# A new order and new engines for the same operations in a one-core matmul kernel

## The chip, the cores and the metric

The kernel runs on one core of one Trainium2 chip. The metric is device time in microseconds (us) of one execution; lower is better. The engines are named as the profile names them: PE (TensorE, matmuls), PEld (its weight loads), DVE (VectorE), ACT (ScalarE), POOL (GpSimd), SP (SyncE, which here only issues DMAs). SBUF is the on-chip memory, PSUM the banks that PE writes its results to.

## The reference

For 4 batch rows of 1024 tokens with 512 features, in float32:

```
hidden   = concat(cond, cond)                              # (4, 512)
fused    = concat(x, mean_over_tokens(x), hidden)          # (4, 1024, 1536)
out      = x + relu(fused @ W + b)                         # W: (1536, 512)
```

Mean and hidden do not depend on the token, so for batch row r the matmul splits into `x @ W[0:512]` and one bias row `mean(x_r) @ W[512:1024] + cond_r @ (W[1024:1280] + W[1280:1536]) + b`.

## The kernel before, in words

**Products.** Tokens are cut into 32 tiles of 128 (t0 to t31, eight to a batch row). Each float32 operand is split into a rounded high part (`hi`, `w_hi`) and the rest (`lo`, `w_lo`), and a tile's result is the sum of hi\*w_hi, lo\*w_hi and hi\*w_lo over four blocks j of 128 features: 12 matmuls of 128x512 into one PSUM bank (`p{t}.{j}`, line 366; t31 goes in two halves of 256 columns, 24 matmuls). In the order table `p0.2.1` is one of the three alone, n = 0, 1, 2 in the order above. Tile t uses bank t mod 5, so tile t+5 needs tile t's bank emptied.

**Units.** The x operand has to be transposed. Tiles come in units u0 (t0), u1 (t1), u2 (t2, t3) and then u3 to u9 of four tiles. The first three are transposed by PE (`T`, line 261) from a regrouped copy (`y`, lines 237 and 239); from u3 on DVE transposes (`T`, line 263) what a DMA `Z{u}.{i}` brought into `z`: two of the four blocks into PSUM (`px`), the odd two into SBUF (`xT`). Then ACT writes `h` (the high part, and its sum over tokens, line 270), and `l` writes the rest, xT or px minus hi (line 276), on DVE or POOL; POOL cannot take the px blocks. The weights are split the same way (`wh`, `wl`, lines 218 to 224).

**Bias of a batch row r.** ACT scales the folded condition weights (`g`), POOL adds them up (`d`), ACT copies that into the PSUM tile `acc` (`as`). POOL turns the sums over tokens into means (`to`, lines 308 to 311); DVE adds mean times weight in four steps (`m{r}.0` to `m{r}.3`, line 320); then ACT `f`, DVE `fa`, ACT `vh`, DVE `vl` (lines 328 to 340) fold and split the result, one matmul `pb{r}` (line 344) sums it over partitions, and ACT copies it to `bias` (`bc`, line 348). `pb{r}` stands in PE's own stream between products: if `vl{r}` is late, PE waits.

**After the products.** Tiles t0 to t11: `K` empties the bank (ACT or DVE), `b` adds the bias in SBUF (line 437). Tiles t12 to t27: DVE's `K` empties the bank and adds the bias (line 441). Then `r` is the relu (line 446 on DVE, 448 on ACT), `F` adds x (line 455, DVE or POOL), `S` stores the tile. Tiles t28 to t31: `P` puts the bias into the bank beforehand, and DVE's `F` (lines 404, 424) does relu and sum from PSUM in one operation.

**What sets the order.** The string `ORDER` lists every operation once; `@d`, `@a`, `@p` give the engine (DVE, ACT, POOL) where there is a choice. The kernel is recorded in this order, each engine runs its own operations strictly in it, and waits go in from the data and buffers used. All DMAs but the first two of the weights go through SP in the order of the table, so an SP issue that waits holds the ones behind it.

Of the kernel before, what the change touches and what calls it, by code (L numbers as in the profile page):

```python
# [19 lines left out]


ORDER = """
W0@a fill W1@a X0.0 X0.1 W2 fill relu fill W3 fill X0.2 fill Z3.1 fill y0.1@d y0.0@p y0.2@p fill T0.0 wh0r@d Z3.2
T0.1 T0.2 wh0l@d h0.0 fill wl0r@p fill y1.0@d y1.1@a T0.3 l0.0@d fill h0.2 wl0l@p fill h0.1 T1.2 T1.0 p0.0.1 T1.1
wh1@d Z3.3 T1.3 p0.0.0 h1.0 p0.0.2 Z3.0 h1.3 l1.0@d p1.0.2 wl1@p h1.2 l0.1@d p1.0.0 l1.3@d wh2@a p0.1.0 p1.0.1 wh3@d
h1.1 p0.1.1 p0.2.0 h0.3 l0.2@d wl2@p C p1.2.0 l1.1@d p1.3.1 V p0.3.0 p1.1.0 B y3.0@d y2.0@a p1.3.0 p0.2.1 Z4.0
l1.2@d p1.1.1 wl3@d p1.1.2 p0.2.2 T2.2 Z4.2 T2.3 p1.2.1 h2.2 T2.0 T2.1 l2.2@d p0.3.2 Z4.3 h2.0 p1.2.2 p3.2 h2.3
l2.0@d h2.1 l2.3@d p2.0 l2.1@d Z4.1 l0.3@d p2.3 p2.2 T3.0 p3.1 T3.3 h3.0 T3.1 p3.0 h3.3 l3.0@d p2.1 h3.1 l3.3@p t3
p3.3 T3.2 M1 K2@d p1.3.2 l3.1@p M0 p0.3.1 K1@a p4.0 t2 M2 h3.2 p0.1.2 ac0@p p6.0 M3 l3.2@d K0@a p4.3 Z5.2 t0 K3@d
p5.3 t1 Z5.3 ac1@d g0.0 p7.2 p6.2 d0.0 Z5.0 g0.1 p5.2 d0.1 g1.0 p5.0 Z5.1 T4.1 T4.3 p5.1 d1.0 T4.2 p6.3 K5@a Z6.0  # L30
T4.0 as0 p4.2 to0 g1.1 p7.3 Z6.3 h4.1 m0.0 p6.1 g2.0 l4.1@p m0.1 p4.1 Z6.2 h4.2 m0.2 p7.1 K4@a m0.3 h4.3 p7.0 Z6.1
K6@a p8.1 l4.3@p l4.2@d h4.0 X4.1 p10.1 f0 Z7.2 d1.1 p9.1 fa0 Z7.1 p10.3 l4.0@d vh0 d2.0 p8.2 g2.1 vl0 Z7.0 p11.2
K7@a T5.3 d2.1 p11.3 T5.2 h5.3 Z7.3 p8.0 T5.0 l5.3@p T5.1 pb0 p10.0 bc0@a h5.0 p10.2 b1@p h5.1 X1.1 l5.0@d p9.3 X2.0
h5.2 b2@d p9.0 as1 Z8.2 to1 p9.2 r1@a l5.1@p l5.2@d p12.3 r2@a X1.0 m1.0 K9@a p8.3 Z8.0 F1@p T6.3 p11.0 T6.1 h6.3
p12.2 b0@p m1.1 h6.1 p12.0 T6.2 K8@a p12.1 b3@p g3.0 T6.0 p11.1 K10@a m1.2 Z9.3 h6.2 d3.0 p13.1 Z8.3 m1.3 h6.0 p14.0
Z8.1 l6.0@d f1 b4@p p13.3 r0@a l6.2@d p14.1 r3@a T7.2 l6.3@p p15.0 fa1 Z9.2 p13.0 T7.0 vh1 F2@p p15.1 K11@a vl1 X5.0
p13.2 F0@d Z9.0 b6@p p15.2 S1 T7.3 pb1 X5.1 l6.1@p p14.3 bc1@a as2 p14.2 K13 F3@p r6@a p16.0 K12 h7.3 p15.3 K14 h7.2
l7.3@p T7.1 p17.0 b5@d h7.1 p19.3 b9@p h7.0 p17.3 r4@a l7.0@d p19.2 to2 g3.1 l7.2@d F4@p p16.2 r5@a m2.0 p18.3 K15
b8@p S4 p18.2 Z9.1 m2.1 p16.3 X3.1 d3.1 m2.2 p19.0 m2.3 p18.1 F5@p T8.0 p16.1 f2 fa2 p20.3 b11@p S5 T8.3 S2 p17.2
vh2 X3.0 h8.0 vl2 p17.1 F6@p X2.1 h8.3 S3 T8.2 p19.1 l7.1@d b7@p S6 p20.0 X4.0 pb2 S0 p18.0 bc2@a l8.3@p X7.0 h8.2  # L40
p20.2 K17 r7@a p20.1 K16 as3 F7@p p22.2 T8.1 l8.0@d p21.3 h8.1 T9.0 S7 r8@a p21.1 l8.1@p X6.1 K19 r11@a p22.1 r9@a
l8.2@d b10@p p22.0 r14@a K18 p21.2 r13@a T9.1 h9.0 p24.2 F13@p T9.2 h9.1 p24.1 T9.3 h9.2 F8@p F9@d p21.0 r15@a p24.0
r10@a F11@p S8 K20 h9.3 p22.3 S13 K21 r17@a p23.1 X6.0 to3 r21@a p23.0 F10@p m3.0 r18@a p23.3 r20@a m3.1 p26.1
l9.3@p m3.2 p25.0 K22 F21@p p23.2 m3.3 r22@a p26.2 F15@p f3 S21 p24.3 S11 r12@a fa3 p27.3 S10 F17@p K23 S15 vh3
p25.1 S9 r16@a vl3 p25.2 r19@a F16@p r23@d p26.0 l9.0@d p25.3 F19@p S16 pb3 X7.1 p26.3 bc3@a S17 F12@p P28 p27.1 K25
p27.2 l9.2@d P30 F18@p p28.2 F14@d r25@a p30.2 l9.1@p K26 p28.0 S14 S18 F25@d P31l p27.0 S19 F23@p r26@a p30.0 K24
S25 p31.2l F26@p S23 K27 p31.0l r24@a S12 p31.1l P29 p31.3l F20@p p30.3 P31r F31l F22@d S31l p29.1 S26 p28.1 S20
r27@d S22 p29.0 F24@d F27@p p28.3 p29.3 F28 S24 p30.1 S27 S28 p29.2 F30 p31.1r F29 S30 p31.0r p31.3r S29 p31.2r F31r
S31r
""".split()  # L50


# [437 lines left out]
```

## Time and profile before

| | |
|---|---|
| median of 3 runs | 102.46 us (102.29 to 104.08) |
| the profiled execution | 102.85 us, span 101.1 us |
| PE busy | 95.8 us (95%), 427 matmuls |
| DVE / ACT / POOL busy | 79.3 / 60.6 / 80.0 us |
| HBM | 18.88 MB read, 8.39 MB written |

The span runs from the first instruction to the last; 1.75 us of the profiled execution lie around it. Matmuls overlap, so PE's busy share does not tell whether it lost time: the step from one matmul's start to the next one's does.

### The profile page before, as it was taken

The page shows a single profiled execution, that of the slowest core. Times are in us where ns is not written, and L with a number is a line of the kernel's source. Part 1 is how long each engine was busy: PE and PEld are TensorE (multiplying, and loading weights), DVE is VectorE, ACT ScalarE, POOL GpSimd, SP SyncE. Part 2 cuts the span into 40 slices and gives each one's busy share as a digit, 9 for nine tenths or more (in the row PEclk, how much of TensorE's full clock was granted, in tenths as well). Part 3 has the DMA queues.
Part 4 walks back from the last instruction along what each step waited for, and adds up shares of the span by engine and source line. Part 5 has one row for each costly group of instructions (what it writes and reads, how often), then busy time and mean ns, then how long its engine had stood idle before and what let it go on. Part 6 is the DMA issues. An engine that isn't in the chain of part 4 may idle for free.

```text
span 101.1 us, 1437 instructions
## 1 busy us (share of the span) xinstructions
PE 95.8 (95%) x427; PEld 76.4 (76%) x427; DVE 79.3 (78%) x129; ACT 60.6 (60%) x150; POOL 80.0 (79%) x77
## 2 busy tenths in 40 slices
PE   6999999999999999999999999999999998999940
PEld 2476888888888888888878888888878885898840
DVE  1257658984897889987999999989859799969930
ACT  2574545844996698993597327499955786350000
POOL 5359000969769899999999999999899999999700
PEclk9999999999999999999999999999999999999999
DMA  2999999999999999999999999999999759998894
GB/s 46 372 343 227 210 211 316 205 205 322 207 199 191 210 223 197 206 260 298 241 225 209 207 254 307 265 359 408 405 397 400 274 219 345 282 403 328 310 381 161
DMA packets 25345, 27.36 MB, mean 271 GB/s; under 512 B 1397, under 2 KB 15993, under 8 KB 25338
## 3 DMA queue, kind: packets, MB, share of 16 engines
q1 hardware_dynamic: 25050, 26.75, 102.6%
q10 hardware_dynamic: 288, 0.52, 1.5%
q8 instruction: 3, 0.05, 0.2%
q14 instruction: 4, 0.03, 0.1%
HBM read 18.88 MB, written 8.39 MB: 270 GB/s over the span
## 4 chain that ended last, share of the span: by engine, by line
PE 38%; DMA 23%; POOL 18%; DVE 10%; ACT 4%; issue 2%; ACTq 1%; SPq 1%; POOLq 0%
PE po L366 37%; DMA z<-in_x_dram 9%; POOL x L455 8%; DMA x<-in_x_dram 8%; DMA x<-in_L_cond_W_dram 6%; POOL lo L276 4%; POOL o L437 4%; DVE acc L320 2%; DVE lo L276 2%; ACT hi L270 2%; DVE w_hi L220 1%; DVE o L446 1%; POOL cond L302 1%; DVE o L441 1%; PE px L261 1%
## 5 line engine op out<-in xcount | busy, mean ns | idle before, releaser
L366 PE MATMUL po<-w_hi,lo 128*128 128x512 f32 (+1 forms) x132 | 50.7, 387 | 0.5 <-DVE lo L276 0.4
L366 PE MATMUL po<-w_hi,hi 128*128 128x512 f32 (+1 forms) x132 | 50.2, 385 | 0.0
L366 PE MATMUL po<-w_lo,hi 128*128 128x512 f32 (+1 forms) x132 | 50.1, 385 | 0.0
L455 POOL TENSOR_TENSOR x<-o,x 128x512 f32<-128x512 f32 x22 | 30.0, 1385 | 0.7 <-DVE o L446 0.4
L366 PEld LDWEIGHTS po<-w_hi,lo 128*128 128x128 f32 x132 | 24.8, 188 | 6.1 <-DVE lo L276 0.8
L366 PEld LDWEIGHTS po<-w_hi,hi 128*128 128x128 f32 x132 | 24.8, 188 | 5.4 <-DVE o L441 0.6
L366 PEld LDWEIGHTS po<-w_lo,hi 128*128 128x128 f32 x132 | 24.7, 188 | 5.0 <-ACT hi L270 0.3
L276 POOL TENSOR_TENSOR lo<-xT,hi 128x512 fp32r<-128x512 f32 x13 | 17.7, 1367 | 9.2 <-ACT hi L270 9.2
L448 ACT ACTIVATE o<-o 128x512 f32<-128x512 f32 x26 | 15.2, 622 | 4.0 <-DVE o L441 3.4
L437 POOL TENSOR_TENSOR o<-o,bias 128x512 f32<-128x512 f32 x10 | 13.9, 1390 | 0.0
L276 DVE TENSOR_TENSOR lo<-px,hi 128x512 fp32r<-128x512 f32 (+2 forms) x20 | 11.5, 588 | 2.2 <-ACT hi L270 2.2
L270 ACT ACTIVATE hi<-px 128x512 fp32r<-128x512 f32 (+2 forms) x20 | 10.3, 517 | 4.8 <-DVE px L263 2.5
L320 DVE SCALAR_TENSOR_TENSOR acc<-w_mean,tot,acc 128x512 f32<-128x512 f32 x16 | 12.0, 748 | 1.4 <-POOL tot L311 1.1
L441 DVE TENSOR_TENSOR o<-po,bias 128x512 f32<-128x512 f32 x16 | 10.5, 679 | 1.6 <-POOL x L455 1.4
L263 DVE STREAM_TRANSPOSE xT<-z 128x512 f32<-128x512 f32 x14 | 9.4, 687 | 2.2 <-POOL cond L302 2.2
L263 DVE STREAM_TRANSPOSE px<-z 128x512 f32<-128x512 f32 x14 | 9.5, 699 | 2.0 <-DMA z<-in_x_dram 1.8
L270 ACT ACTIVATE hi<-xT 128x512 fp32r<-128x512 f32 x14 | 8.7, 624 | 1.8 <-DVE xT L263 1.7
L455 DVE TENSOR_TENSOR x<-o,x 128x512 f32<-128x512 f32 x6 | 7.2, 1194 | 0.0
L298 ACT ACTIVATE term<-wc,cT 128x512 f32<-128x512 f32 x8 | 5.7, 718 | 2.2 <-DVE cT L284 1.4
L433 ACT ACTIVATE o<-po 128x512 f32<-128x512 f32 x10 | 5.9, 590 | 0.8 <-PE po L366 0.8
L302 POOL TENSOR_TENSOR cond<-b_sb,term 128x512 f32<-128x512 f32 x4 | 5.2, 1292 | 1.0 <-ACT term L298 1.0
L224 POOL TENSOR_TENSOR w_lo<-x,w_hi 128x256 fp32r<-128x256 f32 (+1 forms) x4 | 4.2, 1068 | 1.8 <-DVE w_hi L220 1.8
(60 smaller groups left out, 74.0 us busy)
## 6 DMA issues: line engine op xcount, KB each, us to landing
out_dram<-x SPq DMA_DIRECT2D x31, 256.0 KB, 3.2
x<-in_x_dram SPq DMA_DIRECT2D x15, 512.0 KB, 8.8
z<-in_x_dram SPq DMA_DIRECT2D x28, 256.0 KB, 9.6
x<-in_L_cond_W_dram SPq DMA_DIRECT2D x1, 1024.0 KB, 9.4
w_mean<-in_L_cond_W_dram SPq DMA_DIRECT2D x4, 256.0 KB, 8.2
x<-in_L_cond_W_dram ACTq DMA_DIRECT2D x2, 256.0 KB, 4.6
x<-in_x_dram SPq DMA_DIRECT2D x2, 256.0 KB, 2.8
x<-in_L_cond_W_dram SPq DMA_DIRECT2D x2, 256.0 KB, 5.5
```

The costliest lines, as they stand in the source:

```text
L263: nc.vector.transpose(xT.rearrange("p (n q e) -> p n q e", q=Q // E, e=E), zs[z_of(u)][:, : n * NQ].rearrange("p n (q j e) -> p n j q e", ...
L270: nc.scalar.activation(his[buf][:, col : col + m], xT, AF.Copy, accum_out=sums[:, r, j, s : s + 1])
L276: nc_of[e].tensor_tensor(los[buf][:, col : col + m], xT, his[buf][:, col : col + m].bitcast(F32), ALU.subtract)
L298: nc.scalar.activation(terms[k], wc[:, k], AF.Copy, scale=cT[:, k, r : r + 1])
L302: nc.gpsimd.tensor_tensor(conds[r % 2], conds[r % 2] if k else b_sb, terms[k], ALU.add)
L320: nc.vector.scalar_tensor_tensor(acc, w_mean[:, j, :], tot[:, r, j : j + 1], acc, ALU.mult, ALU.add)
L366: nc.tensor.matmul(v, lhsT=a[:, col : col + P], rhs=m, start=WAYS[t] != "I" and key not in done, stop=done.count(key) == 3 * J - 1, skip_g ...
L433: nc.scalar.activation(o, bank(t), AF.Copy)
L437: nc_of[e].tensor_tensor(o, o, biases[r], ALU.add)
L441: nc.vector.tensor_tensor(o, bank(t), biases[r], ALU.add)
L448: nc.scalar.activation(o, o, AF.Relu)
L455: nc_of[e].tensor_tensor(x_tile(t), o, x_tile(t), ALU.add)
```

## The change

Only the string `ORDER` differs. No operation is added or removed, and buffers, shapes and code stay. The order of nearly everything moves a little, and these change engine:

| operation | DVE before, after | POOL before, after | ACT before, after |
|---|---|---|---|
| `F` (adds x, SBUF only) | 6, 11 | 22, 17 | |
| `b` (adds bias, SBUF only) | 2, 4 | 10, 8 | |
| `r` (relu, SBUF only) | 2, 1 | | 26, 27 |
| `l` of an xT block, u3 on (SBUF only) | 1, 5 | 13, 9 | |
| `wl` (half and whole blocks of the weights) | 1, 4 | 4, 1 | |
| `wh` (the same) | 4, 3 | | 1, 2 |
| `y` (regrouped copies of t0 to t3) | 3, 2 | 2, 0 | 2, 5 |

```diff
-W0@a fill W1@a X0.0 X0.1 W2 fill relu fill W3 fill X0.2 fill Z3.1 fill y0.1@d y0.0@p y0.2@p fill T0.0 wh0r@d Z3.2
...
+W0@a fill W1@a X0.0 X0.1 fill W2 fill relu W3 fill fill X0.2 fill Z3.1 y0.1@a fill y0.0@a y0.2@a fill fill wh0l@d
```

**The start, on PE.** Before, the last of the eleven warm-up matmuls (line 134, on `warm`) and the first products (line 366; `o11` is tile 0's regrouped copy, `o10` tile 1's, and line 261 transposes them):

```order
L134 LDWEIGHTS warm_130
L134 MATMUL po2_138<-warm_130 128x512
L261 MATMUL po3_139<-term1_123,o10_113 128x128
L261 MATMUL acc_143<-term1_123,o10_113 128x128
L366 MATMUL po0_136<-w_hi_72,lo0_89 128x512
L261 MATMUL acc_143<-term1_123,o10_113 128x128
L261 MATMUL po3_139<-term1_123,o10_113 128x128
L366 MATMUL po0_136<-w_hi_72,hi0_75 128x512
L366 MATMUL po0_136<-w_lo_73,hi0_75 128x512
```

Now:

```order
L134 LDWEIGHTS warm_130
L134 MATMUL po2_138<-warm_130 128x512
L261 MATMUL po4_140<-term1_123,o11_114 128x128
L261 MATMUL px0_141<-term1_123,o11_114 128x128
L261 MATMUL acc_143<-term1_123,o10_113 128x128 x2
L261 MATMUL px1_142<-term1_123,o11_114 128x128
L261 MATMUL po3_139<-term1_123,o10_113 128x128 x2
L366 MATMUL po0_136<-w_hi_72,hi0_75 128x512
L366 MATMUL po1_137<-w_lo_73,hi1_76 128x512
```

Before, seven warm-up matmuls stood ahead of the first transpose and four between the transposes; now all eleven stand ahead of it, and seven of the eight transposes ahead of the first product.

**The bias of row 1, on DVE.** Before, the stretch that ends with `vl1` (line 340) and the operation behind it:

```order
L276 TENSOR_TENSOR lo_91<-px_141,hi_77 128x512
L276 TENSOR_TENSOR lo_93<-px_142,hi_79 128x512
L263 STREAM_TRANSPOSE px_142<-z_70 128x512
L332 TENSOR_TENSOR acc<-acc,fold 64x512
L263 STREAM_TRANSPOSE px_141<-z_70 128x512
L340 TENSOR_TENSOR v_acc<-acc,v_acc 64x512
L455 TENSOR_TENSOR x_65<-o_103,x_65 128x512
```

Now:

```order
L437 TENSOR_TENSOR o_107<-o_107,bias_115 128x512
L263 STREAM_TRANSPOSE px_142<-z_69 128x512
L263 STREAM_TRANSPOSE xT_120<-z_69 128x512
L320 SCALAR_TENSOR_TENSOR acc<-w_mean,tot,acc 128x512 x2
L263 STREAM_TRANSPOSE px_141<-z_69 128x512
L276 TENSOR_TENSOR lo_93<-px_142,hi_79 128x512
L332 TENSOR_TENSOR acc<-acc,fold 64x512
L263 STREAM_TRANSPOSE xT_121<-z_69 128x512
L276 TENSOR_TENSOR lo_92<-xT_120,hi_78 128x512
L437 TENSOR_TENSOR o_110<-o_110,bias_115 128x512
L340 TENSOR_TENSOR v_acc<-acc,v_acc 64x512
```

`b4` (o_107) stands ahead of the last two mean steps, and `l6.1` (lo_92) and `b7` (o_110), both on SBUF alone, stand between `fa1` and `vl1`; the transposes of u7 that stood there have moved behind.

**The bias of row 3, on DVE.** Now, from the first mean step (line 320) to what follows `vl3`:

```order
L320 SCALAR_TENSOR_TENSOR acc<-w_mean,tot,acc 128x512 x3
L441 TENSOR_TENSOR o_112<-po_137,bias_117 128x512
L320 SCALAR_TENSOR_TENSOR acc<-w_mean,tot,acc 128x512
L332 TENSOR_TENSOR acc<-acc,fold 64x512
L455 TENSOR_TENSOR x_68<-o_104,x_68 128x512
L441 TENSOR_TENSOR o_114<-po_139,bias_117 128x512
L340 TENSOR_TENSOR v_acc<-acc,v_acc 64x512
L455 TENSOR_TENSOR x_63<-o_109,x_63 128x512
L455 TENSOR_TENSOR x_64<-o_111,x_64 128x512
L276 TENSOR_TENSOR lo_89<-px_141,hi_75 128x512
```

Before:

```order
L320 SCALAR_TENSOR_TENSOR acc<-w_mean,tot,acc 128x512 x3
L441 TENSOR_TENSOR o_113<-po_138,bias_117 128x512
L320 SCALAR_TENSOR_TENSOR acc<-w_mean,tot,acc 128x512
L332 TENSOR_TENSOR acc<-acc,fold 64x512
L441 TENSOR_TENSOR o_114<-po_139,bias_117 128x512
L340 TENSOR_TENSOR v_acc<-acc,v_acc 64x512
L446 TENSOR_SCALAR o_114<-o_114 128x512
L276 TENSOR_TENSOR lo_89<-px_141,hi_75 128x512
L441 TENSOR_TENSOR o_104<-po_136,bias_118 128x512
L276 TENSOR_TENSOR lo_91<-px_142,hi_77 128x512
```

`F13` (x_68) has come in between `fa3` and `vl3`, and `F18` and `F20` follow; before, only `K23` (o_114) stood between them, and `l9.2`, which now runs before the first mean step, came after a relu behind `vl3`.

## Rows read from the trace of the kernel before

**Rows 1.** The page's part 1: busy us (share of the span) xinstructions.

```profile
PE 95.8 (95%) x427; PEld 76.4 (76%) x427; DVE 79.3 (78%) x129; ACT 60.6 (60%) x150; POOL 80.0 (79%) x77
```

**Rows 2.** The chain that ended last, in order of time: start, length, what.

```profile
12.31 22.94 PE po L366 x101
...
85.43 11.81 PE po L366 x62
```

**Rows 3.** Timeline of PE: start, length, instruction [idle before <-releaser].

```profile
0.97 3.17 PE L134 MATMUL po<-warm 128*128 128x512 bf16 x7 [0.97 <-DVE one L126]
...
4.64 0.88 PE L134 MATMUL po<-warm 128*128 128x512 bf16 x2
...
5.47 0.59 PE L134 MATMUL po<-warm 128*128 128x512 bf16 x2
...
6.04 0.48 PE L366 MATMUL po<-w_hi,lo 128*128 128x512 f32 x1
...
12.61 0.40 PE L366 MATMUL po<-w_hi,hi 128*128 128x512 f32 x1
...
75.05 0.39 PE L366 MATMUL po<-w_lo,hi 128*128 128x512 f32 x1
75.42 0.50 PE L366 MATMUL po<-w_hi,hi 128*128 128x512 f32 x1
...
84.69 0.39 PE L366 MATMUL po<-w_hi,hi 128*128 128x512 f32 x1
```

**Rows 4.** Timelines of DVE and ACT in the start, same columns.

```profile
6.95 0.43 DVE L220 CAST w_hi<-x 128x512 fp32r<-128x512 f32 x1 [1.04 <-DMA x<-in_L_cond_W_dram]
7.89 1.15 DVE L220 CAST w_hi<-x 128x512 fp32r<-128x512 f32 x1
10.09 0.43 DVE L239 COPY o<-x 128x512 f32<-128x512 f32 x1 [0.65 <-DMA x<-in_x_dram]
10.09 0.64 ACT L237 ACTIVATE o<-x 128x512 f32<-128x512 f32 x1 [1.51 <-DMA x<-in_x_dram]
```

**Rows 5.** Groups by line and shape: count | busy us, mean ns | idle before.

```profile
L455 DVE TENSOR_TENSOR x<-o,x 128x512 f32<-128x512 f32 x6 | 7.2, 1194 | 0.0
L276 DVE TENSOR_TENSOR lo<-xT,hi 128x512 fp32r<-128x512 f32 x1 | 1.1, 1073 | 0.0
L446 DVE TENSOR_SCALAR o<-o 128x512 f32<-128x512 f32 x2 | 3.0, 1490 | 0.0
L292 DVE TENSOR_TENSOR wc<-x 128x512 f32<-128x512 f32 x1 | 0.7, 694 | 0.0
```

**Rows 6.** Timelines of DVE and POOL, where an `F` on DVE meets POOL.

```profile
49.12 1.47 DVE L455 TENSOR_TENSOR x<-o,x 128x512 f32<-128x512 f32 x1
51.14 1.84 DVE L441 TENSOR_TENSOR o<-po,bias 128x512 f32<-128x512 f32 x3
...
48.76 1.29 POOL L437 TENSOR_TENSOR o<-o,bias 128x512 f32<-128x512 f32 x1
50.00 1.75 POOL L276 TENSOR_TENSOR lo<-xT,hi 128x512 fp32r<-128x512 f32 x1
```

**Rows 7.** Stages (from `T5.3` to `F31r`'s end, four in all): length, busy (count) by engine.

```profile
33.75:48.40 14.65, 14.65 (x66) 12.17 (x65) 13.09 (x20) 11.55 (x30) 14.12 (x13) 1.00 1.16 233
48.40:75.80 27.40, 27.40 (x121) 22.25 (x121) 24.69 (x35) 18.76 (x45) 26.88 (x25) 1.00 1.11 299
...
sum 63.94, PE 63.12 PEld 51.77 DVE 56.97 ACT 39.69 POOL 60.47; mean PE 15.78 PEld 12.94 DVE 14.24 ACT 9.92 POOL 15.12
```

**Rows 8.** Timeline of DVE around row 3's bias.

```profile
74.08 1.29 DVE L441 TENSOR_TENSOR o<-po,bias 128x512 f32<-128x512 f32 x2 [1.19 <-POOL x L455]
75.80 2.34 DVE L320 SCALAR_TENSOR_TENSOR acc<-w_mean,tot,acc 128x512 f32<-128x512 f32 x3 [0.44 <-POOL tot L311]
...
81.40 0.68 DVE L340 TENSOR_TENSOR v_acc<-acc,v_acc 64x512 fp32r<-64x512 f32 x1
84.70 0.67 DVE L276 TENSOR_TENSOR lo<-px,hi 128x512 fp32r<-128x512 f32 x1
```

More of the change, by code (lines that the diff above doesn't have):

```diff
@@ L22 @@
 ORDER = """
-W0@a fill W1@a X0.0 X0.1 W2 fill relu fill W3 fill X0.2 fill Z3.1 fill y0.1@d y0.0@p y0.2@p fill T0.0 wh0r@d Z3.2
[L24 to L47, printed above, removed]
@@ L48 @@
-r27@d S22 p29.0 F24@d F27@p p28.3 p29.3 F28 S24 p30.1 S27 S28 p29.2 F30 p31.1r F29 S30 p31.0r p31.3r S29 p31.2r F31r
-S31r
+W0@a fill W1@a X0.0 X0.1 fill W2 fill relu W3 fill fill X0.2 fill Z3.1 y0.1@a fill y0.0@a y0.2@a fill fill wh0l@d
+Z3.3 fill wl0l@d fill y1.1@a y1.0@d T0.2 T0.0 wh0r@d T1.0 wl0r@d T1.1 h0.0 T0.1 T1.2 h1.0 T1.3 p0.0.0 h1.1 l1.0@d
+p1.0.2 h1.2 l0.0@d p1.0.0 l1.1@d h1.3 p1.0.1 l1.2@d h0.1 p0.0.1 Z3.0 wh1@d T0.3 wh2@a p0.0.2 l1.3@d Z3.2 p1.1.0
+wl1@d p1.1.1 wh3@a p1.2.1 wl2@p l0.1@d p0.1.0 h0.3 p1.3.1 h0.2 l0.3@d p1.3.0 p0.1.2 p0.3.0 B p1.1.2 p1.2.2 C p0.2.0
@@ new lines @@
+p0.1.1 V y3.0@a y2.0@d p0.2.2 p0.3.1 wl3@d Z4.1 T2.2 T2.3 l0.2@d T2.0 h2.2 T2.1 Z4.3 p1.2.0 h2.3 l2.2@d p0.2.1
+p1.3.2 l2.3@d p3.2 K1@a Z4.0 h2.1 p3.3 h2.0 l2.1@d p2.3 l2.0@d Z4.2 p0.3.2 p3.1 K0@d p2.1 T3.1 p3.0 T3.0 h3.1 T3.3
+p2.0 h3.0 l3.1@d h3.3 p2.2 t3 p5.1 l3.0@d M1 K2@a T3.2 M2 p6.1 t2 M0 h3.2 p4.0 l3.3@d M3 t1 p6.0 to0 Z5.2 p7.3 ac0@d
+ac1@p p5.3 t0 Z5.1 l3.2@d g0.0 p4.1 K3@d d0.0 g0.1 Z5.3 p4.3 p7.1 d0.1 g1.0 T4.3 Z5.0 p6.2 T4.2 p5.0 d1.0 as0 T4.1
+p5.2 Z6.0 h4.3 T4.0 p7.0 h4.2 l4.3@p p6.3 h4.1 Z6.2 l4.2@d p7.2 m0.0 l4.1@p K6@a Z6.1 g1.1 p4.2 m0.1 p8.3 d1.1 m0.2
@@ new lines @@
+K4@a Z6.3 K7@a p11.1 m0.3 g2.0 p8.2 K5@a Z7.3 d2.0 p9.1 h4.0 p8.1 f0 l4.0@d Z7.1 g3.0 p11.2 fa0 g2.1 p11.0 T5.3 Z7.0
+vh0 T5.1 d2.1 p9.0 h5.3 vl0 p10.2 h5.1 T5.0 l5.3@p p8.0 T5.2 h5.0 p10.3 l5.1@p Z8.0 h5.2 l5.0@d pb0 Z8.3 p10.1
+l5.2@d bc0@a Z7.2 as1 p9.2 to1 b5@d K8@a p12.3 Z8.2 b0@d p12.0 b6@p m1.0 r0@a p10.0 X2.0 m1.1 Z8.1 p11.3 K10@a b4@d
+r6@a p12.2 b2@p T6.2 r5@a p9.3 T6.1 p12.1 F0@p m1.2 K9@a g3.1 p13.0 m1.3 r2@a d3.0 p13.3 T6.0 h6.2 p14.1 f1 l6.2@d
+b1@p p14.3 h6.1 fa1 p15.3 r4@a T6.3 vh1 p14.0 l6.1@d Z9.2 h6.0 p15.2 Z9.0 b7@d r1@a X4.0 F2@p p15.1 vl1 h6.3 X1.0 S0
@@ new lines @@
+T7.2 p13.2 K11@a X3.0 l6.3@p l6.0@d p14.2 X1.1 T7.1 Z9.1 pb1 p13.1 S2 T7.0 b3@p bc1@a as2 p16.1 K14 h7.1 p16.3 X3.1
+T7.3 h7.0 K12 p15.0 h7.2 F1@d p19.2 h7.3 l7.1@p K13 S1 p16.2 r3@a X4.1 p16.0 Z9.3 to2 p19.1 F3@p m2.0 p19.0 m2.1
+X2.1 d3.1 p18.1 m2.2 p17.1 m2.3 l7.3@p p17.3 l7.0@d f2 p17.0 r7@a K15 b11@p p18.0 fa2 p19.3 F4@d vh2 p17.2 b9@p T8.1
+S4 p18.2 vl2 b8@p l7.2@d p20.1 T8.3 pb2 p20.0 bc2@a F6@d r11@a p18.3 F5@p K16 r8@a p20.2 T8.2 p21.2 F8@p S5 K17 X6.0
+p20.3 K18 r17@a X5.1 F7@d h8.1 S6 p22.3 X5.0 b10@p T8.0 h8.3 p22.2 K19 r16@a p23.0 l8.1@d r10@a p21.3 l8.3@p h8.2
@@ new lines @@
+T9.1 p23.3 h8.0 l8.2@d p24.1 h9.1 F16@p T9.2 p22.0 r9@a T9.3 p22.1 l8.0@d F10@p S16 h9.3 K20 p21.0 as3 T9.0 h9.2
+F9@p S10 p24.3 K22 h9.0 p21.1 l9.2@d r22@a S9 p25.0 to3 S3 r15@a F11@p m3.0 p23.2 X7.0 r18@a m3.1 p27.1 r19@a F15@p
+p25.2 m3.2 p23.1 K21 F19@p S15 p25.3 m3.3 S11 S7 p27.2 F17@p f3 S19 p25.1 r13@a fa3 r14@a p24.0 F13@d vh3 F14@p
+p26.2 K23 S13 r20@a S8 vl3 p26.0 r12@a X7.1 r21@a F18@d p27.0 F20@d p24.2 F21@p l9.0@d S20 pb3 X6.1 p27.3 bc3@a S17
+l9.3@p P28 p26.3 K25 S14 S18 p26.1 K27 P30 p28.2 F12@d r25@a r27@a K24 p28.0 P31r l9.1@d p28.3 r23@a F22@d P29
@@ L50 @@
+p31.2r p31.3r F23@d r24@a S22 p30.3 F25@p K26 S23 p28.1 S21 P31l S12 p31.1r F27@p F28 S25 p30.2 p31.0r F24@d S27
+p29.2 S28 r26@d p29.1 S24 F26@p p29.3 p30.0 S26 p30.1 p29.0 F30 p31.1l F31r S30 p31.0l F29 S31r p31.3l p31.2l S29
+F31l S31l
 """.split()
```

## The prediction, made before the change was run

> **What bounds the kernel now.** I read the busy shares first, then the chain that ended last, then PE's timeline by the step between starts, and last what DVE and POOL do where PE loses time. PE is busy 95% [rows 1]; the chain gives 22.94 us for 101 products [rows 2], 0.227 us each. That is the step of a PE that waits for nothing, and from 12.6 us on nearly every step is that long. The exceptions: 0.37 us from 75.05 to 75.42 [rows 3], where a bank was emptied late because DVE's `K20` had waited 1.19 us for POOL [rows 8], and 0.74 us from 84.69 to 85.43 [rows 2, 3], where `l9.2`, at 84.70 [rows 8], came late. Each first step after a wait is some 0.1 us longer, so these places cost 0.25 and 0.63 us, about 0.9 together. The rest of PE's loss lies in the first 12.6 us. So this is a PE-bound kernel, and the change can only win what PE now waits for: little. DVE and POOL decide what it can lose. From 33.75 us, when u5's transposes begin, to the end of the last operation on DVE at 97.69, a stretch of 63.94 us, DVE is busy 56.97 and POOL 60.47 [rows 7].
>
> **The start.** Seven warm-up matmuls take 3.17 us from 0.97, the two at 4.64 take 0.88 and the two at 5.47 only 0.59 [rows 3]: a step of some 0.43 us that halves between 5.1 and 5.5. All eleven now run first: ten at 0.43 (to 5.25), one at 0.22, so the first transpose comes at 5.45 and, with seven at 0.11, the first product at about 6.3, against 6.04 [rows 3]. It has one transpose left to do instead of two. What then held PE goes: the fourth block's `wh` took 1.15 us on DVE [rows 4] beside POOL's `wl` and is now ACT's, and the first `wl`, POOL's before, runs on DVE right behind the `wh` it needs. Weight block 1 still allows `wh1` at 6.95 + 0.43 [rows 4], but six products now need block 0 alone, and 6.3 + 6 x 0.23 lies beyond 7.4, so nobody waits. The next gate is u2: its x lands at 10.07, shown by both copies starting at 10.09 [rows 4], and the same transfers stand ahead of it on SP in both kernels. Its copies are done at 10.7. In the new order 20 products and the transpose stand ahead of u2's transposes: 6.3 + 20 x 0.227 + 0.11 + 0.1 for one wait = 11.05. Eight transposes (0.9) and three products (0.7) bring `p3.2`, the first product of u2, to about 12.6. Before it started at 12.61 [rows 3] with 21 of the 24 products of u0 and u1 done; now 23 are. Gain: two products, 0.45 us. Bounds: nothing if the new order waits twice, 0.8 if nothing waits and the transposes start at 10.75.
>
> **If PE then never waits:** 0.45 + 0.9 less about 0.05 for a slow step or two = 1.3, at most 1.5. It ends at 97.25 now (85.43 + 11.81, [rows 2]), so at 95.75 to 95.95.
>
> **DVE's load.** In the stretch of 63.94 us DVE gets five more `F`, two more `b`, two more `l` of xT blocks (the other two are u3's, earlier) and one `r` less. Alone, such an operation takes 0.694 us (`ac1`, run while POOL was idle) [rows 5]; back to back operations step by 1.84 / 3 = 0.61 [rows 6]. Beside POOL it takes more: six `F` 1.194 on average, the `l` 1.073, the `r` 1.490 [rows 5]. The mechanism stands in one place [rows 6]: `F0` starts at 49.12, while POOL's `b` runs from 48.76 to 50.05; it ends at 50.59, 0.54 after that one, and POOL's next operation, begun at 50.00, takes 1.75 instead of 1.29. So each waits out what the other has begun: DVE pays about 0.5 us on average, POOL 0.45. The Trainium skill, "SBUF — State Buffer", section "Who interferes with whom", says the same as a rule: a VectorE operation with two inputs in SBUF and a GpSimd operation that reads SBUF exclude each other, and the second to issue blocks fully until the first is done. By that rule a DVE operation that always meets POOL halfway through would wait 0.65 us where I take 0.5 or less, and the 18 operations with two inputs would cost some 3 us more than in my sum; it speaks against moving work to DVE while POOL is kept busy.
>
> Sum: the eleven of before paid 6 x 0.50 + 2 x 0.5 + 0.38 + 2 x 0.9 (the `r`) = 6.2 us of contention inside the 56.97. Without it DVE has 50.8; the eight operations more (nine at 0.61, less one `r` at 0.6) make 55.7. Contention of the new 19 lies between 0 and 18 x 0.5 + 0.9 = 9.9: DVE needs 55.7 to 65.6 us. It has 62.6 if PE never waits. I take 0.3 each, near 5.5 in all and nearer the lower half, because POOL loses nine operations of 1.24 (its step, 48.76 to 50.00, [rows 6]) in the stretch, 11 us, and gets 8 x 0.45 = 3.6 of waits back: 60.5 falls to 53, 83% instead of 95%, so it is met less often. That gives DVE 61.2 of 62.6 us: it fits, with hardly any idle time, and before it idled 7.0 us. So it will be late at some of PE's gates.
>
> **Gate 1: `pb1`.** From `p3.2` PE runs 163 products and `pb0` before `pb1`: 12.6 + 164 x 0.227 = 49.8 us. From 33.75, set by the same landings, DVE has to do 23 operations up to `vl1` (before: the 20 in [rows 7] and `vl1`): 23 x 0.61 + 0.4 for the mean steps that follow each other = 14.4, so 48.2 without any wait. Five of them (`b5`, `b0`, `b4`, `l6.1`, `b7`) can meet POOL: 0 to 2.5 us; the old stretch idled 14.65 - 13.09 = 1.56 [rows 7]. So `vl1` ends between 48.2 and 52.2. With 1.2 and 0.8 it is 50.2, and PE waits 0.4 us.
>
> **Gate 2: `pb3`.** 307 steps after `p3.2`: 82.3. From the first mean step of row 3 to `vl3` took 75.80 to 82.08 [rows 8]; `F13`, now between `fa3` and `vl3`, adds 0.6 (0 if it hides behind ACT's step, 1.2 if it meets POOL). So `m3.0` has to start by 75.4, 25.6 after gate 1. Now 39 operations stand between, five more than before: 39 x 0.61 + 0.5 = 24.3 us without waits; five can meet POOL (`F1`, `F4`, `F6`, `F7`, `l8.1`), 0 to 2.5, and the old stretch idled 27.40 - 24.69 = 2.7 [rows 7]. With 1.2 and 0.7 that is 26.2: late by 0.6. Behind gate 2, `l9.2` no longer comes late; `F18` and `F20` now stand ahead of `l9.0`, which PE needs some 3 us after `pb3`, so I cost them at nothing, or 0.5 if both meet POOL.
>
> Transfers are costed at nothing: the same bytes, z ahead of x in the new order; SP's one new hold is u9's last z behind the store of t1, whose `F1` is due near 55, ten us before the transposes that need it. Of ACT the moved `wh`, `y` and `r` are cheap: it idles 24 us of the 63.94 [rows 7]. The stores and the end behind the last product have the same shape (a half of 256 columns, one DMA) and stay.
>
> **Forecast.** PE: -1.35 for start and old waits, +0.4 + 0.6 for the gates, less 0.3, since a wait at gate 1 gives DVE that time at gate 2: -0.65 or so. The profiled execution took 102.85, 0.39 above the median of 102.46, so it would be 102.2; against the median **101.8 us**. Its own range, by gates that cost 0.3 to 1.7 together: 101.4 to 102.8.
>
> **Rivals.** *DVE keeps up:* the 19 operations fall into POOL's gaps, no gate costs anything, -1.3 to -1.5: 101.0 us, at best (0.8 from the start) 100.6. For it: POOL's load falls by 7 us. Against: the six `F` of before took 1.194 on average, so most of them met it [rows 5].
> *DVE just full:* 0.45 us of contention each and 1 us of waits on ACT make 55.7 + 8.5 + 1 = 65.2 us from 33.75, and the last `F` ends at 98.95 instead of 97.69: 103.7 us; it reaches from 102.8 to 104.4. For it: POOL is still busy five sixths of the time.
> *DVE becomes the bound:* every one of the 19 pays as before (65.6) and DVE keeps 2.5 of its 7.0 us idle, since `f`, `vh` and `h` on ACT have to answer it four times: 68.1 us, the end at 101.85, +4.2: 106.6 us. It decides from some 66 us of DVE on, idle time included; gate 1 would then cost 2 us. By the Trainium skill's rule (the same section, 0.65 us each) DVE would be busy 68 us, and the time 106.6 without any idle time.
> *The change does nothing:* the start gains nothing and gate 2 takes back what the old waits gave: 102.5 us, inside the forecast's range.
>
> **Chances.** Forecast 0.47; DVE keeps up 0.23; just full 0.19; DVE the bound 0.11. The measurement tells about 2% (2.05 us): faster means under 100.4, slower over 104.5. Under 100.4 needs more than PE's known waits, so a quarter of the second case at most: 0.06. Over 104.5: the last case and a little of the third, 0.12. Same: 0.82. Range 100.5 to 104.0: it leaves out the last case and the ends, under 2 in 10.
>
> **What would show it.** First product at about 6.3 us and `p3.2` near 12.6; no PE step over 0.3 at the places of 75.4 and 85.4; DVE's `F` and `b` below 1.1 us on average and POOL's share near 83% in the stretch; PE's remaining waits just ahead of line 344 (`pb1`, `pb3`), ended by DVE's line 340. It is wrong if the first product comes before 6.0 or after 6.6, if `F` on DVE still takes 1.2, if PE waits elsewhere for over 1 us (a bank, or a z that lands late), or if DVE idles 5 us or more and PE still waits.

## The result and the profile after: 1.4% slower, where 0.6% faster was forecast

The changed kernel takes 103.64 us (median) against 102.43 for the kernel before. The ratio is 1.0139 [1.0101, 1.0177], so 1.0 to 1.8 us are lost where the forecast had 0.65 to win. Some executions of either kernel run some per cent longer than the rest; every ratio here leaves these out, so it can differ from that of two medians.

The profiled execution took 103.49 us with a span of 101.47. The busy shares, to be read against [rows 1]:

```profile
PE 96.1 (95%) x427; PEld 76.3 (75%) x427; DVE 81.5 (80%) x140; ACT 62.5 (62%) x155; POOL 63.3 (62%) x61
```

POOL lost 16.7 us of work and DVE gained only 2.2, though it has eleven operations more: the aim of the table of engines was met. PE's share is the same, which says nothing about a kernel that PE bounds. The chain that ended last (start, length, what) tells more:

```profile
0.97 4.86 PE po L134 x11
...
12.72 0.93 PE po L366 x4
13.67 16.63 PE po L366 x72
...
63.94 0.38 DVE x L455
64.31 1.09 issue
65.40 0.69 DVE o L441
66.13 18.08 PE po L366 x78
84.22 0.23 PE acc L344
84.44 13.20 PE po L366 x69
97.66 0.42 DVE x L404
```

From 66.13 us to the last product the chain is PE's, and ahead of that it runs back through DVE, a DMA, SP and ACT to 30.30 us, where PE's own part ends; within that part it has a hole before 13.67 us. The old stalls of [rows 2, 3] near 75 and 85 us are gone, and PE passes `pb3` (line 344) without a gap. PE's timeline has the rows that answer to [rows 3] (start, length, instruction, idle before and what ended it):

```profile
6.50 0.50 PE L366 MATMUL po<-w_hi,hi 128*128 128x512 f32 x1
...
7.94 0.48 PE L366 MATMUL po<-w_lo,hi 128*128 128x512 f32 x1
8.36 0.47 PE L366 MATMUL po<-w_hi,hi 128*128 128x512 f32 x1
...
13.25 0.39 PE L366 MATMUL po<-w_hi,hi 128*128 128x512 f32 x1
13.67 0.50 PE L366 MATMUL po<-w_hi,lo 128*128 128x512 f32 x1
...
14.94 0.39 PE L366 MATMUL po<-w_hi,hi 128*128 128x512 f32 x1
...
50.75 0.39 PE L344 MATMUL acc<-v_acc,ones 128*128 128x512 f32 x1
...
65.26 0.39 PE L366 MATMUL po<-w_lo,hi 128*128 128x512 f32 x1
66.13 0.50 PE L366 MATMUL po<-w_hi,hi 128*128 128x512 f32 x1 [0.49 <-DVE o L441]
```

Steps of 0.42 us stand where 0.227 is even: 7.94 to 8.36 (`p1.1.0`) and 13.25 to 13.67 (within `p3.2`). The third long step, 65.26 to 66.13, is 0.87. On DVE and then POOL, the instructions behind these three:

```profile
7.79 0.42 DVE L220 CAST w_hi<-x 128x512 fp32r<-128x512 f32 x1
...
13.19 0.76 DVE L276 TENSOR_TENSOR lo<-px,hi 128x256 fp32r<-128x256 f32 x2 [1.20 <-ACT hi L270]
...
63.86 1.62 DVE L455 TENSOR_TENSOR x<-o,x 128x512 f32<-128x512 f32 x1
65.40 0.68 DVE L441 TENSOR_TENSOR o<-po,bias 128x512 f32<-128x512 f32 x1
```

```profile
63.62 1.31 POOL L455 TENSOR_TENSOR x<-o,x 128x512 f32<-128x512 f32 x1
```

`wh1` starts at 7.79, 0.84 later than in [rows 4], because four `l` of tiles 0 and 1 now stand ahead of it on DVE. `l2.2`, the first of the two at 13.19, waits for `h2.2` on ACT and so for `T2.2` on PE. And `F6` on DVE starts 0.24 us after POOL's `F5` and takes 1.62 us; `K16` stands behind it, and `p21.2` needs the bank that `K16` empties.

I profiled the kernel before a second time. There PE starts its 30th product at 14.50 us; in the changed kernel that is the row at 14.94. So the start lost 0.44 us. The long step at 65 us with its slower successor costs 0.76, the old stall at 84.3 (0.36 in that second trace, none near 75) is gone, and steps that are longer by less than 0.1 each make up the rest of the difference at PE's end, 97.62 against 96.59. From there to the end of the span both need 3.85 us. The last part lies outside the span: 103.49 - 101.47 = 2.02 us against 102.21 - 100.44 = 1.77. In all +1.28.

### The profile page after: what moved, and what is told of

Same layout as the page of the kernel before. It is cut to its first block, busy times and chain, and to the rows that moved or that the text cites. A ratio compares the mean times of both kernels' runs of the same rounds, so it can differ in the third digit from the quotient of the medians.

```text
span 101.5 us, 1447 instructions
## 1 busy us (share of the span) xinstructions
PE 96.1 (95%) x427; PEld 76.3 (75%) x427; DVE 81.5 (80%) x140; ACT 62.5 (62%) x155; POOL 63.3 (62%) x61
## 4 chain that ended last, share of the span: by engine, by line
PE 60%; DVE 17%; DMA 8%; issue 4%; SPq 4%; ACT 3%; DVEq 0%
PE po L366 53%; DMA z<-in_x_dram 8%; PE po L134 5%; DVE xT L263 4%; SPq L148 4%; DVE lo L276 3%; DVE o L437 3%; DVE px L263 2%; ACT o L433 2%; DVE acc L320 1%; DVE v_acc L340 1%; ACT hi L270 1%; PE px L261 1%; DVE x L455 1%; DVE acc L332 1%
## 5 line engine op out<-in xcount | busy, mean ns | idle before, releaser
L366 PE MATMUL po<-w_hi,hi 128*128 128x512 f32 (+1 forms) x132 | 51.1, 387 | 0.5 <-DVE o L441 0.5
L366 PE MATMUL po<-w_hi,lo 128*128 128x512 f32 (+1 forms) x132 | 50.5, 385 | 0.0
L366 PE MATMUL po<-w_lo,hi 128*128 128x512 f32 (+1 forms) x132 | 50.3, 384 | 0.0
L366 PEld LDWEIGHTS po<-w_hi,hi 128*128 128x128 f32 x132 | 24.8, 188 | 6.3 <-DVE o L441 0.9
L366 PEld LDWEIGHTS po<-w_hi,lo 128*128 128x128 f32 x132 | 24.8, 188 | 5.6 <-DVE lo L276 0.9
L366 PEld LDWEIGHTS po<-w_lo,hi 128*128 128x128 f32 x132 | 24.8, 188 | 4.9
L455 POOL TENSOR_TENSOR x<-o,x 128x512 f32<-128x512 f32 x17 | 23.7, 1404 | 4.3 <-ACT o L448 3.3
L448 ACT ACTIVATE o<-o 128x512 f32<-128x512 f32 x27 | 15.8, 621 | 2.4 <-DVE o L441 2.0
L276 POOL TENSOR_TENSOR lo<-xT,hi 128x512 fp32r<-128x512 f32 x9 | 11.6, 1295 | 3.9 <-ACT hi L270 3.8
L437 POOL TENSOR_TENSOR o<-o,bias 128x512 f32<-128x512 f32 x8 | 11.3, 1430 | 0.0
L455 DVE TENSOR_TENSOR x<-o,x 128x512 f32<-128x512 f32 x11 | 8.8, 816 | 0.0
L308 POOL TENSOR_TENSOR pre<-sums 128x8 f32<-128x8 f32 x1 | 0.2, 250 | 11.4 <-ACT hi L270 11.4
L302 POOL TENSOR_TENSOR cond<-cond,term 128x512 f32<-128x512 f32 x4 | 5.2, 1295 | 1.8 <-ACT term L298 1.7
```

The costliest lines, as they stand in the source:

```text
L276: nc_of[e].tensor_tensor(los[buf][:, col : col + m], xT, his[buf][:, col : col + m].bitcast(F32), ALU.subtract)
L302: nc.gpsimd.tensor_tensor(conds[r % 2], conds[r % 2] if k else b_sb, terms[k], ALU.add)
L366: nc.tensor.matmul(v, lhsT=a[:, col : col + P], rhs=m, start=WAYS[t] != "I" and key not in done, stop=done.count(key) == 3 * J - 1, skip_g ...
L437: nc_of[e].tensor_tensor(o, o, biases[r], ALU.add)
L448: nc.scalar.activation(o, o, AF.Relu)
L455: nc_of[e].tensor_tensor(x_tile(t), o, x_tile(t), ALU.add)
```

## The experiments

Unless it is told otherwise, an experiment edits the string `ORDER` alone, and ratios are to the kernel before, run beside it. The edited files are a text line shorter, so L365 there is L366 here.

**The change once more, unaltered.**

> The changed kernel unaltered, a second time. If its slow start belongs to the order (theory: start), the first product is again near 6.5 us, the x of u2 lands again near 10.7, and p3.2 begins near 13.2 to 13.7; if the 10.74 was a chance of that execution, it lands near 10.1 as before. Time 103.5 to 103.7, 1.2 us over the kernel before.

1.0149 [1.0072, 1.0227]: the time repeats, and the long step near 65 us is there again (0.86 us). The start does not: the first product comes at 5.93 us, the x of u2 lands at 11.4 and `p3.2` begins at 13.79, so these three move between executions of one kernel.

**The two halves.** The new order up to u4's first transpose and the old one behind it, and the reverse (what was done in the other half is left out of the second):

```diff
 ... d0.1 g1.0
-T4.3 Z5.0 p6.2 T4.2 p5.0 d1.0 as0 T4.1 p5.2 Z6.0 h4.3 ...   (the changed order's rest)
+p7.2 p6.2 Z5.0 p5.2 p5.0 T4.1 T4.3 d1.0 T4.2 p6.3 K5@a ...   (the old order's rest)
```

> The new order up to the first transpose of u4 (about 24 us), then the old order for all the rest. Theory start: the traces put 0.5 us of the loss ahead of 13.7 us, and the old waits (0.25 and 0.63 us at 75 and 85) stay, so 102.9 to 103.3. Theory DVE (the operations moved to DVE cost the time): the rest is the old one, so 102.4, the same as before.

> The old order up to the first transpose of u4, then the new order for all the rest. Theory start: the rest of the new order loses 0.76 us at K16 and saves 0.88, so 102.2 to 102.5, not slower than before. Theory DVE: nearly all the loss stays, 103.3 to 103.7.

Measured: 1.0311 [1.0262, 1.0361] with the new start, 1.0141 [1.0079, 1.0204] with the new rest. The first lies outside both theories; the second is about what theory DVE named, and the next run tests that theory. PE in the kernel with the new start:

```profile
29.32 0.39 PE L365 MATMUL po<-w_lo,hi 128*128 128x512 f32 x1
30.10 0.50 PE L365 MATMUL po<-w_hi,hi 128*128 128x512 f32 x1 [0.39 <-ACT hi L269]
31.45 0.50 PE L365 MATMUL po<-w_hi,lo 128*128 128x512 f32 x1 [0.85 <-POOL lo L275]
```

Steps of 0.78 and 1.35 us: the seam itself stalls. The old rest wants row 0's bias chain earlier than the new start delivers it: DVE idles 2.99 us for ACT's `as0` before `m0.0` at 28.83, and u4's `h` and `l` come late behind that. So this run says nothing on what the new start costs with its own rest. The other says that the old start does not mend the change: the loss does not lie in the start alone.

**`F6` behind `K16`.**

```diff
-bc2@a F6@d r11@a p18.3 F5@p K16 r8@a
+bc2@a r11@a p18.3 F5@p K16 F6@d r8@a
```

> The new order with one operation moved: F6 on DVE, which waited out POOL's F5 (1.62 us at 63.86) ahead of K16, now behind K16. Theory collision: PE's 0.88 us step at 65.3 shrinks to 0.23, and as no other step of PE is long behind 14 us, the whole 0.65 to 0.76 us comes off: 102.8 to 103.0. Theory DVE full: DVE is busy 27.0 of 27.4 us there, so the wait returns at the next gate and 103.4 to 103.7 stay.

1.0101 [1.0051, 1.0151], a median of 103.32 us: by the time alone the second theory is the nearer one. DVE and the chain of this kernel say otherwise:

```profile
63.82 0.69 DVE L440 TENSOR_TENSOR o<-po,bias 128x512 f32<-128x512 f32 x1 [0.31 <-ACT bias L347]
64.43 0.68 DVE L454 TENSOR_TENSOR x<-o,x 128x512 f32<-128x512 f32 x1
```

```profile
13.94 23.37 PE po L365 x103
37.31 0.23 PE acc L343
37.54 12.92 PE po L365 x57
50.46 0.23 PE acc L343
50.68 12.24 PE po L365 x54
62.92 0.23 PE acc L343
63.15 20.06 PE po L365 x87
83.21 0.23 PE acc L343
83.44 13.23 PE po L365 x69
```

`K16` waits for ACT's bias alone, `F6` behind it meets nobody (0.68 us), and from 13.94 us PE's chain has no hole: all four `pb` stand in it without a wait. That settles two things. The long step came from the collision: with 0.68 us for `F6` in its old place `K16` would have ended near 65.1 us, ahead of the 65.5 at which PE wanted the bank. And no theory of a full DVE is left, since in this trace PE waits for DVE nowhere behind 14 us. Yet the kernel stays slower: PE ends at 96.66, as early as in the second trace of before, but 4.46 us pass from there to the end of the span, not 3.85.

**The kernel before once more, for its trace.**

> The kernel before, unaltered, for a second trace. Two of its numbers decide how much of the slow start is chance. Theory start: p3.2 begins near 12.6 us with 21 of the first 24 products done, whatever the landings do. Theory chance: the step of the warm-up matmuls and the landing of u2's x move by 0.5 us or more and p3.2 with them. The step at 84.7 us (0.75) should come back, 0.6 to 0.8; the end behind the last product should be 3.8 to 3.9 us again. Time 102.2 to 102.9.

1.0000 [0.9973, 1.0028]. SP's waits from 80 us on tell the two orders of stores apart (queue, line <- engine, tile, line waited for: us in total, times, longest). Before, then the changed kernel:

```profile
SPq L148 <- POOL x L455: 4.4, 5, 1.6
...
SPq L148 <- DVE x L455: 1.6, 1, 1.6
```

```profile
SPq L148 <- DVE x L455: 5.4, 4, 2.8
```

One wait of 2.8 us is new: SP stands at `S22` from 87.5 to 90.4 us, until `F22` is done on DVE, and holds `S21` behind it, whose `F21` POOL had done by 86.3. Then nine stores go out one behind the other, up to 95.9 us. The DMA view from 88 us on (KB each, median us from issue to landing), before and changed:

```profile
out_dram<-x SPq DMA_DIRECT2D x11, 256.0 KB, 2.4
```

```profile
out_dram<-x SPq DMA_DIRECT2D x11, 256.0 KB, 3.3
```

**`S21` ahead of the wait,** alone and with `F6`:

```diff
-K25 S14 S18 p26.1 ... S23 p28.1 S21 P31l
+K25 S14 S18 S21 p26.1 ... S23 p28.1 P31l
```

> The new order with only the store of t21 moved ahead of those of t22, t23 and t12 on SP; F6 stays ahead of K16. Theory tail: the store line alone costs 0.4 to 0.6 us, so 0.9% over the kernel before instead of 1.4%; PE keeps its 0.8 us step at K16. Theory collision only: all that f6_s21 won came from F6, and this stays at 1.4%.

> The new order with F6 behind K16 and, on SP, the store of t21 moved ahead of those of t22, t23 and t12. In the run with F6 alone PE ended at 96.66 us but the last store was issued 0.71 us after its data was ready, because SP and the DMA engines were still busy with ten stores issued back to back. Theory tail: with one store earlier SP is free in time, the end behind the last product shrinks from 4.46 to about 3.9 us, and the time falls by 0.4 to 0.6, to 0.5 over the kernel before. Theory landing: the DMA engines and not SP's place in line set the end, then at most 0.1 is won.

1.0046 [1.0012, 1.0080] alone, 1.0035 [0.9992, 1.0078] with `F6`. Alone, the long step stays (0.88 us), PE ends at 97.45 and the span 3.52 us later, 0.33 less than in the change. So the place of one store costs 0.9% by the two ratios, more than the one trace shows. The traces don't show the loss alike: in the first one of the changed kernel SP was free when the last store's data was there (98.08 us, issued at 98.11), and the 3.85 us behind PE's end are those of before; its second trace has 4.41, the one with `F6` moved 4.46. `F6` beside `S21` is worth 0.1% and alone 0.4%, which the intervals can't tell apart.

**SP's hold at 41 us.** The chain of the changed kernel passes through SP from 48 us, since `Z9.2` waits 7.2 us for a buffer of u6 and holds x loads. In this run `Z9.2` and `Z9.0` come later:

```diff
-Z9.2 h6.0 p15.2 Z9.0 b7@d ... X1.1 T7.1
+h6.0 p15.2 b7@d ... X1.1 Z9.2 Z9.0 T7.1
```

> The same, and on SP the loads Z9.2 and Z9.0, whose buffer is free only after u6's last transpose and which held SP from 41 to 48 us with the DMA engines nearly idle, moved behind X1.1. Theory hold: the 7 us in which hardly anything was moved come back as a full DMA at the end; moving them lets x in earlier, the last ten stores land faster (2.3 to 2.7 us instead of 3), and the time falls by another 0.3 to 0.6. Theory harmless: no x is waited for in this trace, so nothing changes (within 0.2).

1.0036 [1.0001, 1.0071]: no difference from 1.0035, though 0.13 us more lie outside the span here (see below). The longest wait on SP costs nothing that could be measured; in this trace PE waits for nothing but its first operand.

**The old start with both repairs.**

> The old order up to the first transpose of u4, then the new one with F6 behind K16 and the store of t21 moved. Theory start (the new start costs 0.5 us): 0.4 to 0.6 below f6_s21, so equal to the kernel before or up to 0.5 faster. Theory chance: as f6_s21, within 0.2.

1.0029 [1.0001, 1.0058], the edits being those of the new rest above, `F6` and `S21`: within the intervals of the new start with both repairs. Going back to the old start won nothing that could be measured.

**What lies outside the span.** Sixteen memsets of one column on DVE, about 0.06 us each, in the kernel before:

```diff
 nc.vector.memset(sums, 0.0)
+pad = sb("pad", [P, 1])
+for _ in range(16):
+    nc.vector.memset(pad, 0.0)
```

> The kernel before with 16 memsets of one column added on DVE at the start, where DVE idles (some 1 us up to about 3 us; its first copy is at 3.5). In all traces so far the time minus the span is 1.77 to 1.79 us where DVE has up to 178 instructions and 2.02 to 2.14 where it has 182 or more, with no waiting engine to explain it. Theory length: with 184 instead of 168 the difference becomes 2.0 to 2.1 and the time 0.25 to 0.35 us longer, at an unchanged span. Theory chance: 1.78 again and no change.

1.0046 [1.0007, 1.0085], and the time outside the span grew from 1.77 to 2.16 us. So longer code on DVE adds time that no view of the span shows. It goes in steps: 1.7 to 1.8 us with 129, 132 and 137 operations on DVE, 2.0 to 2.1 with 140, 2.16 with 145. One kernel breaks this: that with `Z9.2` moved has 140 operations and 2.15. Counted with what DVE's queue executes beside them (its waits, for one), DVE has 168 to 178 instructions in the first group, 182 in the second, and 184 with the memsets and with `Z9.2` moved, so it is this count that the steps follow. The count over all engines (1437 to 1445, 1447 and 1448, 1449 and 1453) orders the kernels in the same way, and no run tells the two apart. Of the change's loss 0.25 us is this. Why it grows was not tried.

**The old stall alone.** The kernel before with `l9.2` right behind `vl3`:

```diff
-vl3 p25.2 ... p27.2 l9.2@d P30
+vl3 l9.2@d p25.2 ... p27.2 P30
```

> The old order with l9.2 moved up on DVE, ahead of the relu r23 and right behind vl3. Theory of the prediction (the step at 84.7 us is PE waiting for l9.2): the step becomes 0.23 us and 0.25 to 0.63 us come off, 0.2 to 0.6% under the kernel before. Theory next in line: l9.0, P30 or a store is late instead and nothing is won.

0.9977 [0.9937, 1.0016]: the stall that the forecast wanted to win back is worth 0.2%, or nothing.

**The start repaired.** `wh1` ahead of `l1.1` on DVE, and two products moved behind u2's transposes, so that `T2.2` comes earlier. On top of `F6` and `S21`, measured twice, then without them, and with `S21` alone:

```diff
-l1.1@d h1.3 p1.0.1 l1.2@d h0.1 p0.0.1 Z3.0 wh1@d T0.3
+wh1@d l1.1@d h1.3 p1.0.1 l1.2@d h0.1 p0.0.1 Z3.0 T0.3
...
-p0.2.2 p0.3.1 wl3@d Z4.1 T2.2 T2.3 l0.2@d T2.0 h2.2 T2.1
+wl3@d Z4.1 T2.2 T2.3 l0.2@d T2.0 h2.2 T2.1 p0.2.2 p0.3.1
```

> f6_s21 with two edits to the start: wh1 goes ahead of the third and fourth split of tile 1 on DVE, and u2's transposes run on PE two products earlier. Theory start: the steps of 0.42 us ahead of p1.1.0 and in p3.2 go, 0.3 to 0.5 us come off f6_s21: equal to the kernel before. Theory landing: the gate is the landing of u2's x and the total is unchanged, 0.3 to 0.4% over the kernel before.

> The changed order with only the start repaired (wh1 ahead of l1.1 on DVE, u2's transposes two products earlier on PE); F6 and S21 stay as in the change. Theory 'three separate faults': the steps of 0.42 us at p1.1.0 and in p3.2 go, so 0.3 to 0.7 us of 1.3 come back: ratio 1.007 to 1.011, the long step near 65 us and the store line stay. Rival 'the store line is the one fault and the start only adds chance': the end behind the last product is set by SP's backlog, a start that is earlier shortens nothing at the end: ratio 1.012 to 1.016. Third, 'the repaired start is what won all': 1.003 or less.

> The changed order with the start repaired and the store S21 moved, F6 left ahead of K16. Known: S21 alone 1.0046, all three 0.9963. Theory 'F6 is worth nothing beside S21' (the 0.7 us step near 65 us is given back later, since PE meets an old wait less): 0.995 to 0.998, like all three. Rival 'F6 costs its 0.7 us still': 1.001 to 1.004.

> The kernel with all three repairs (start, F6, S21) once more on the same chip as its neighbours. If it is better than before its ratio lies at 0.993 to 0.998 again and the two together exclude 1; if the first measurement was luck it lies at 1.000 to 1.004, where the change without the start's repair lay.

All three repairs: 0.9963 [0.9921, 1.0004] and, again, 1.0027 [0.9990, 1.0065]. The start alone: 1.0083 [1.0046, 1.0120]. With `S21` (`s21_start`): 1.0071 [1.0030, 1.0112]. The last three of these ratios come from another chip than the first, with the kernel before beside them. Both steps of 0.42 are gone in the traces of the last three. In that of the start alone another long step came (POOL, DVE and PE):

```profile
7.69 1.29 POOL L223 TENSOR_TENSOR w_lo<-x,w_hi 128x512 fp32r<-128x512 f32 x1 [5.79 <-ACT w_hi L217]
7.74 1.79 DVE L223 TENSOR_TENSOR w_lo<-x,w_hi 128x512 fp32r<-128x512 f32 x1
...
9.59 0.49 PE L365 MATMUL po<-w_lo,hi 128*128 128x512 f32 x1 [0.51 <-DVE w_lo L223]
```

Here `wl1` on DVE began 0.05 us after `wl2` on POOL, took 1.79 us instead of 0.68 and cost PE a step of 0.91. Before, both ran on POOL. In the changed kernel's first trace DVE began 0.01 us ahead (8.33 and 8.34), and POOL took 1.83: which of the two pays is decided by hundredths.

The start as a whole is smaller than its scatter. The 30th product starts at 14.3 to 15.5 us over six traces of the start as changed, at 14.5 to 14.8 over three of the repaired one, and at 14.46 and 14.50 before. By the expectations the start alone speaks for three separate faults. `s21_start` lies above both of its ranges, nearer to the one with a price of `F6` beside the others. The repeat lies where luck was to show; the two runs of all three together give a ratio of 1.000. A weighted fit of three independent effects to the ten ratios of the changed order and its repairs, none of the splices (the run with `Z9.2` moved counts as `F6` and `S21`), gives -0.34% +- 0.28 for `F6`, -0.63% +- 0.30 for `S21` and -0.28% +- 0.26 for the start, from 1.0129: together all of the loss and no more. The fit is loose (`s21_start` lies above `S21` alone), so the single shares are rough.

The version with all three repairs ties with the kernel before; it doesn't beat it. Its chain from the first fill on (the parts in between are PE's too) and its only wait on PE:

```profile
0.97 4.87 PE po L133 x11
...
12.45 25.19 PE po L365 x111
...
83.78 13.20 PE po L365 x69
...
97.01 0.42 DVE x L403
```

```profile
PE po L133 <- DVE one L125: 1.0, 1, 1.0
```

This view lists no other wait of PE, and the time is still that of before. The execution took 103.29 us (the eight behind the ratio have their middle at 102.6), 1.08 more than the second trace of before. Of these, 0.31 are there by the 30th product (14.81 for 14.50; the fills' step halves late, and the first product comes at 6.80 for 6.48), 0.08 come on PE behind it, since small steps (0.33 and 0.34 us near 66.7 and 70.5) take what the old stall gave back, 0.25 lie outside the span, and 0.45 behind PE's end. SP issues the last store 0.03 us after its data in both, but it lands in 2.9 us instead of 2.4. The windows of the last products show why (length, busy us and count of PE, PEld, DVE, ACT, POOL, then the granted clock, DMA share, GB/s), for the second trace of before and for this version:

```profile
92.00:96.00 4.00, 4.00 (x23) 3.45 (x23) 3.81 (x5) 0.00 (x0) 2.62 (x2) 1.00 0.89 328
```

```profile
92.00:96.00 4.00, 4.00 (x22) 3.42 (x21) 2.00 (x5) 0.00 (x0) 1.30 (x2) 1.00 1.05 404
```

Before, the DMA engines have slack there (0.89); in the new order they are full (1.05), and the last store waits for those ahead of it: 4.3 us from PE's end at 96.97 to the end of the span. That is read from the traces; no run moved stores of the whole tail to test it.

## Why the prediction failed, step by step

**What bounds the kernel** held: PE, with about 0.9 us to win in the trace that I had, and 0.4 in the second one. So did the rule that such a change can only win what PE waits for.

**The start failed.** "Nobody waits ... Gain: two products, 0.45 us" became a loss of 0.44 in the one pair of traces (0.28% +- 0.26 by the fit). Two steps were wrong. I held `wh1` against the landing of its weights and the products that don't need it, and not against the four `l` that the order puts ahead of it on DVE: it came 0.84 us later than in [rows 4]. And I let u2's transposes end and its products follow at once, without the way from `T2.2` through ACT's `h` and DVE's `l`. The third term, the fills, was mis-sized: their step halved at 5.6 us, where I took 5.25, and the first product came at 6.50 for a forecast of 6.3. That instant moves by itself: 5.1 to 5.5 in [rows 3], 6.1 in the second trace of before, 4.5 in the second of the changed kernel. The long steps at `p1.1.0` and in `p3.2`, of 0.41 us and more, came back in every trace of the unrepaired start, also where u2's x landed at 9.0 us: they belong to the order.

**The old stalls** went, as forecast (0.25 and 0.63). But they were partly chance: 0.36 in the second trace of before.

**The gates cost nothing,** where I had 0.4 and 0.6. `vl1` ended at 50.12, as forecast (50.2); PE came at 50.75, not 49.8, since it had lost time itself. `vl3` ended at 83.77, and PE came to `pb3` at 84.05, not 82.3. So part of this is luck: by these numbers a PE in time would have waited 0.3 us at the first. In the kernel with `F6` moved PE came at 50.29 and 83.05 and found both ready (49.68 and 82.80).

**Contention** was sized too high. Groups by line and shape answer to [rows 5] (count | busy us, mean ns | idle before):

```profile
L455 DVE TENSOR_TENSOR x<-o,x 128x512 f32<-128x512 f32 x11 | 8.8, 816 | 0.0
L276 DVE TENSOR_TENSOR lo<-xT,hi 128x512 fp32r<-128x512 f32 x5 | 4.5, 909 | 0.0
L437 DVE TENSOR_TENSOR o<-o,bias 128x512 f32<-128x512 f32 x4 | 3.5, 908 | 0.0
```

An `F` on DVE pays 0.12 us on average over the 0.694 of [rows 5], an `l` or `b` 0.22; I took 0.3, and 1.19 was the mean `F` of before. The windows of [rows 7] now:

```profile
33.75:48.40 14.65, 14.65 (x66) 12.15 (x65) 14.39 (x23) 12.93 (x29) 12.94 (x11) 1.00 0.89 187
48.40:75.80 27.40, 26.91 (x119) 21.76 (x118) 26.99 (x41) 16.83 (x43) 21.85 (x18) 1.00 0.98 308
```

DVE is full in both, 41.38 of 42.05 us, as forecast, and of PE's waits only the one at `K16` hangs on it. Over the whole stretch it idles 4.6 us where I had 1.4, and POOL is busy 48.9 us, 76% where I had 83. The rival "just full" names the time that came, 103.7, but not by its way: the end isn't set by DVE.

**What was missing: one collision at a place that counts.** I priced meetings by their mean and set them against two gates. The order keeps nearly all of them harmless behind the start (there, `wl1` with `wl2` can cost as much, as the trace of the start alone shows); one, `F6` with `F5`, stands ahead of a `K` whose bank PE needs at once, and costs 0.76 us of PE. `F6` ends 0.55 us after `F5`, so it waited out the whole rest of it: here the trace agrees with the Trainium skill, "SBUF — State Buffer", "Who interferes with whom" (the second to issue blocks until the first is done). With that price for every operation DVE would have needed 68 us of the stretch of 64; it was busy 59.6 (33.75 to 97.90), and nine of the eleven `F` took under 0.7 us, as if alone.

**What was set at nothing: "the stores and the end ... stay".** By the fit this is the largest share, 0.63% +- 0.30; the three pairs of runs with and without `S21` moved differ by 0.9, 0.7 and 0.1%. SP's line of stores held one that was ready behind one that was not, and what it held came back as a fuller DMA at the end, in some executions more than in others. I compared what the end consists of, and not the order in which SP issues it. The 0.25 us outside the span is a term that the sum didn't have.

## What to carry to other kernels

When a kernel waits for under 1% of its time, a new order can win that at most, and every queue that it reshuffles can lose as much: go through the issue order of each, the stores' too, and ask of each entry what is ready behind it. Price a meeting of engines by what stands behind the instruction that is late, not by the mean of its kind. And take the profile of before twice: of its 0.9 us of stalls, more than half was not there the second time.
